# Choosing the last two sequences' experts together, with four of layer 2's early expert blocks between the last pieces of attention

## The chip, the core and the metric

The kernel runs on one core of one Trainium2 chip. The metric is the device time of one execution in microseconds (us). The kernel before took 618.17 us, the median of 9 runs (616.67 to 621.07).

A core has five engines that the text names as the profile does: PE (matrix products; PEld is its weight load), DVE (element-wise work and reductions), ACT (activations and copies), POOL (here: row scatters and a few powers) and SP (issues transfers).

## The reference

2048 tokens of width 128 (8 sequences of 256), everything in f32. The output is a chain of six residual steps:

```python
x = x + 0.5 * ffn(layernorm(x))                # experts, "layer 1" below
x = x + attention(layernorm(x))                # 16 heads of 8
x = x + 0.5 * ffn(layernorm(x))                # the same experts, "layer 2"
x = x + 0.5 * channel_mix(layernorm(x))
x = x + gated_convolution(layernorm(x))
x = x + 0.5 * channel_mix(layernorm(x))
```

The expert step sends each token to the two best of 8 experts:

```python
h = rmsnorm(x @ W_in.T, in_norm_w)
logits = h @ Wr.T
_, idx = top_k(logits + expert_bias, 2)
gates = softmax over the two chosen logits, 0 elsewhere
for e in range(8):
    oe = rmsnorm(silu(h @ Wg[e].T) * (h @ Wu[e].T) @ Wd[e].T, enorm_w[e])
    out = out + gates[:, e] * oe
return rmsnorm(out, out_norm_w) @ W_out.T
```

The inner width of an expert is 512.

## The kernel before

**Tiles.** The tokens are 16 tiles of 128, four to a chunk (`xs[c]`). Sequence b is half of chunk b // 2. An expert layer has three parts: choosing (`dispatch`, L338), the experts' products (`experts`, L679), and weighing the product rows up (`combine`, L807).

**Choosing.** `dispatch(f, i, parts, mp)` returns the steps for one part of layer f: parts are four tiles each in layer 1 (`EARLY`), and 4, 4, 4, 2, 2 in layer 2 (`LATE`, L58). The steps are `turned` (transposes on PE, copy on ACT), `product` (the matrix product with W_in and Wr together, copied by ACT at L383 to `u`, and its squares at L388), `measured` (statistics of x on DVE), `summed` and `inverted` (the factor `ri` of the norm, L392), `logits` (L407), `scaled` (the two row copies `hrow`, ACT L414), `choice` twice (two rounds of six or seven small DVE operations for all tiles of the part, L416), `ranked` (PE products with `tri` and `ones`, which give each token its row), `placed` (positions `posi`) and `rows` (L465): two scatters on POOL per tile, `hs<-hrow,posi_f` at L470, which lay the rows out by expert in DRAM. For the last two parts of layer 2 the factor is a square root on ACT (L398) and a reciprocal on DVE; for the other parts of layer 2 it is a power on POOL (`power_of`, L170).

**Leading blocks.** For every expert, 128 rows are known to be there before all tokens have chosen (`flagged`, L533, after the first 6 or 8 tiles). These are blocks 0 to 7, one per expert: `weights(e)` fetches an expert's weights (832 KB) to a place set by `homes` or to one of four buffers `w_lead`, `read` (L546) fetches the eight row blocks from `hs`.

**The table.** The rest of the rows make up dynamic blocks, pairs (256 rows, 13 or 12 of them) and singles (128). Which expert and which rows each has is worked out on DVE in seven steps (`table`, L564): counted, summed, paired, spared, singled, named, bounded. `named` writes the row and the expert that SP then reads as registers for its fetches; `bounded` gives the bounds `far`.

**Products.** `work` (L782) runs over leading blocks and then `TURNS[f]` (L48): for each block `gate` (four products on PE, silu on ACT into `sg`), `turn_rows` of the next block, `up` (four products, then `hg = pu * sg` on DVE, L738), then a table step, then `down` of the block before (L740): product `py`, squares on ACT (L762), `yrow` on DVE (L763), two DVE operations for `idx`, and a scatter on POOL for each 128 rows (`y<-yrow_f,idx_f`, L769). Fetches of block i + 3 are issued behind block i, rows before weights. `MORE` blocks run only if the input needs them.

**Order.** PE, DVE, ACT and SP run in the order of the program (a manual schedule), and POOL's marked instructions too. Attention runs in steps s of two halves; `at(s, h, …)` puts pieces of other work behind half "a" or "b" of step s. For layer 2's choosing:

```python
at(33, "a", lead["read"], u6, places, partial(rows, [0]))
at(33, "b", root_table, s6, partial(rows, [1]), w(2))
at(34, "a", partial(turn_back, b), partial(rows, [2]), w(4), i6, l6, c6[0])
at(34, "a", partial(turn_heads, b), partial(rows, [3]), w(2), h6, partial(out_heads, b))
at(34, "a", w(2), x7, w(2), m7, c6[1], u7, w(2), s7, r6)
at(34, "a", i7, p6, rows6, l7, *c7, h7, r7, p7, rows7)
at(34, "a", *(partial(lead["weights"], e) for e in (3, 4, 5)))
```

The suffix 6 marks tiles 12 and 13 (the seventh sequence), 7 marks tiles 14 and 15 (the eighth). x is `turned`, u `product`, m `measured`, s `summed`, i `inverted`, l `logits`, h `scaled`, c the two rounds of `choice`, r `ranked`, p `placed`. `turn_back`, `turn_heads` and `out_heads` (L1069 to L1094) are the last pieces of attention for the last sequence; `out_heads` ends with the addition to x at L1094. `w(n)` is n filler products on PE whose result nobody reads. After this, `second_experts` (L937) fetches the last two leading weights and calls `run_experts` (L891): step `counted` first, then `work` with a table step per leading block, with `named` and `bounded` both at block 4.

Of the kernel before, what the change touches and what calls it, by code (L numbers as in the profile page):

```python
# [2 lines left out]

# [13 lines left out]
P = 128  # L17
# [28 lines left out]
LEAD = 6, 8  # L46
LEADING = list(range(NT, NT + E))
TURNS = (  # L48
    [0, 1, 2, 15, 3, 4, 5, 16, 6, 7, 8, 17, 9, 10, 18, 11],
    [0, 1, 2, 15, 3, 4, 5, 6, 16, 7, 8, 9, 17, 10, 11, 12],  # L50
# [6 lines left out]
EARLY = (0, 4), (4, 4), (8, 4), (12, 4)  # L57
LATE = (0, 4), (4, 4), (8, 4), (12, 2), (14, 2)  # L58
# [15 lines left out]
def macaron_kernel(ctx: ExitStack, tc: tile.TileContext, a: dict, out: bass.AP):  # L74
# [70 lines left out]

    root_table()

# [190 lines left out]
    def dispatch(f, i, parts, mp):  # L338
# [5 lines left out]
        paced = f == 1 and i < len(parts) - 2  # L344
# [4 lines left out]
        def turned():  # L349
            pt = bank(f"pxt_{n}", "sa")  # L350
            for t in range(nt):
                nc.tensor.transpose(pt[:, ts(t, P)], x[:, t, :], ident)
            st["xt"] = xntp.tile([P, CT], F32, tag="xnt", name=f"xnt_{n}")
            nc.scalar.copy(st["xt"][:, 0 : nt * P], pt[:, 0 : nt * P])
            st["u"] = mp.tile([P, TPC, D + E], F32, tag="u", name=f"u_{n}")[:, 0:nt]
            st["ss"] = small.tile([P, nt], F32, tag="ss", name=f"ss_{n}")

        def measured():
            bs = small.tile([P, nt, 6], F32, tag="ast", name=f"ast_{n}")
            mv = small.tile([P, nt, 2], F32, tag="amv", name=f"amv_{n}")  # L360
            for t in range(nt):
                nc.vector.bn_stats(bs[:, t, :], x[:, t, :])
            for t in range(nt):
                nc.vector.bn_aggr(mv[:, t, :], bs[:, t, :])
            st["z"] = small.tile([P, nt], F32, tag="z", name=f"z_{n}")
            nc.vector.tensor_scalar(st["z"], mv[:, :, 1], RMS_EPS, RMS_EPS * LN_EPS, ALU.mult, ALU.add)
# [25 lines left out]
        def summed():  # L392
            ri = small.tile([P, nt], F32, tag="ri", name=f"ri_{n}")
            nc.vector.scalar_tensor_tensor(ri, st["ss"], 1.0 / D, st["z"], ALU.mult, ALU.add)
            if f == 0:
                nc.vector.tensor_copy(hrow[:, :, :, D].bitcast(I32), tokid[:, slots])
            if f == 0 or i >= len(parts) - 2:
                nc.scalar.activation(ri, ri, AF.Sqrt)  # L398
            else:
                power_of(ri, ri, mhalf.to_broadcast([P, nt]))  # L400
            st["ri"] = ri

        def inverted():
            if f == 0 or i >= len(parts) - 2:
                nc.vector.reciprocal(st["ri"], st["ri"])
# [59 lines left out]
        def rows(ts_=range(nt)):  # L465
            for t in ts_:
                if paced:
                    nc.vector.tensor_copy(st["posi"][:, t, :], st["pos"][:, t, :])
                for k in range(2):
# [5 lines left out]
                    )  # L475
                    tc.declare_no_dep(ins.ins, group=f"hs{f}", reason="rows of their own")
# [11 lines left out]
        if i < len(parts) - 2:  # L488
            return turned, *halves, measured, summed, logits, scaled, *choices, both(ranked, placed), rows
        return turned, halves[0], measured, summed, inverted, logits, scaled, *choices, ranked, placed, rows  # L490

    def counts(f):
        pc = bank(f"pcnt_{f}", "sb")[:, 0:E]
# [22 lines left out]

    def leading(f, gp, homes, rows, yrows):
# [6 lines left out]
        lead["taken"], lead["base"], lead["masks"], lead["idx"] = flags[:, 0], flags[:, 1], masks, idx  # L524

# [19 lines left out]

        def read():  # L546
# [5 lines left out]
            for e, row in enumerate(first):  # L552
                hst = rows[e].unsqueeze(1)
# [7 lines left out]
        lead.update(weights=weights, flagged=flagged, read=read)  # L561
# [117 lines left out]
    def experts(f, tab, far, y2, mp, pieces, lead):  # L679
# [3 lines left out]
        hst, w = lead["hst"], lead["w"]  # L683

# [3 lines left out]
        def fetch_weights(t):  # L688
# [3 lines left out]
            e = nc.values_load(tab[0:1, 1, t : t + 1], engines=[SP], min_val=0, max_val=E - 1)  # L692
# [47 lines left out]
        def down(t):  # L740
# [27 lines left out]
            for s in range(m):  # L768
# [10 lines left out]
                if t >= NT:  # L779
                    tc.keep_in_program_order(ins)  # L780
# [961 lines left out]
```

## Time and profile before

| what | us |
|---|---|
| median of 9 runs | 618.17 |
| the profiled execution | 616.43 |
| its span in the trace | 614.6 |
| layer 1, choosing (from the start) | 0 to 50 |
| layer 1, eight leading blocks | 51 to 90.9 |
| layer 1, dynamic blocks | 90.9 to 176 |
| combining and attention | 176 to 375.4 |
| layer 2, rest of the choosing | 375.4 to 393.5 |
| layer 2, eight leading blocks | 393.5 to 420.1 |
| layer 2, dynamic blocks | 420.1 to 503.8 |
| last three steps | 504 to 614.6 |

The profile lists busy times of each engine, the span in 40 slices with the granted clock of PE, the chain of waits that ended last, and groups of equal instructions. A line of the timeline is: start, duration, engine, line of the kernel, operation, out<-in, shapes, and in brackets how long the engine had stood idle before it and what ended that. "remote" and "issue" mark idle time for which the trace shows no releasing instruction of the engines it names. Busy over the whole span: PE 518.9 us (84%), DVE 357.4 (58%), ACT 277.7 (45%), POOL 194.0 (32%). The mean granted clock is 0.933 of full speed.

### The profile page before, as it was taken

The numbers are of one execution on the slowest core, as the hardware profiler recorded it, in microseconds if no ns is written. First come the engines' busy times: TensorE is split into PE (matmuls) and PEld (weight loads), VectorE is DVE, ScalarE is ACT, GpSimd is POOL, SyncE is SP. The second block draws the span as 40 slices with busy tenths as digits, with TensorE's granted clock in tenths as the row PEclk, the third lists the DMA queues.
The fourth block names the chain that finished last, engine by engine and source line by source line (L and its number), as shares of the span: only waits on it lengthen the run. The fifth ranks groups of instructions, "written<-read, shape, count | busy, mean of one in ns | idle before, by whom it ended". The sixth has DMA issues, their size and how long they took to land.

```text
span 614.6 us, 11358 instructions
## 1 busy us (share of the span) xinstructions
PE 518.9 (84%) x3954; PEld 402.8 (66%) x3954; DVE 357.4 (58%) x1129; ACT 277.7 (45%) x683; POOL 194.0 (32%) x202
## 2 busy tenths in 40 slices
PE   6325679999978998899899887589999978879996
PEld 5315679889854645555555554589989964558884
DVE  5643555456433666766876885484444432777675
ACT  4524233222223555666665564333323323885365
POOL 0647324575333111101101435522333434410110
PEclk9556699999989999999999999599999998989999
DMA  8823056766513308218026104617667705000002
GB/s 308 347 67 119 27 190 208 214 189 187 195 28 97 54 28 246 90 44 281 24 63 153 52 24 142 255 32 256 192 192 249 220 24 139 2 0 2 1 0 69
DMA packets 37952, 76.96 MB, mean 125 GB/s; under 512 B 4667, under 2 KB 27106, under 8 KB 36608
## 3 DMA queue, kind: packets, MB, share of 16 engines
q1 hardware_dynamic: 33360, 66.62, 35.0%
q0 software_dynamic: 4528, 9.52, 4.4%
q8 instruction: 35, 0.57, 0.4%
q14 instruction: 29, 0.24, 0.1%
HBM read 55.28 MB, written 21.44 MB: 125 GB/s over the span
## 4 chain that ended last, share of the span: by engine, by line
PE 59%; DVE 14%; ACT 10%; DMA 8%; issue 7%; POOL 1%; SPq 0%; DVEq 0%; ACTq 0%; POOLq 0%
PE pg_f L722 9%; PE ps L1127 9%; PE pu_f L722 9%; PE py_f L745 8%; DMA y<-yrow_f,idx_f 5%; PE po L1174 4%; ACT es L1164 3%; PE pvf L1496 2%; PE pgo L1523 2%; DVE m L1147 2%; PE pm L1110 2%; PE pht_f L709 1%; DMA hst_f<-hs 1%; DMA y_f<-y 1%; PE pk_m L1440 1%
## 5 line engine op out<-in xcount | busy, mean ns | idle before, releaser
L1164 ACT ACTIVATE es<-ps 128x1024 f32<-128x1024 f32 x64 | 65.3, 1021 | 53.0 <-PE ps L1127 28.6
L1147 DVE TENSOR_REDUCE m<-pm 128x4 f32<-128x1024 f32 x64 | 77.5, 1220 | 12.6 <-PE pm L1110 12.6
L1127 PE MATMUL ps<-qa,qk 32*128 32x256 f32 x512 | 72.8, 401 | 12.0 <-ACT es L1164 8.6
L738 DVE TENSOR_TENSOR hg_f<-pu_f,sg_f 128x1024 f32<-128x1024 f32 (+1 forms) x48 | 46.5, 969 | 62.1 <-PE pu_f L722 38.5
L470 POOL DMA_INDIRECT hs<-hrow,posi_f x64 | 61.7, 964 | 62.9 <-issue 25.7
L769 POOL DMA_INDIRECT y<-yrow_f,idx_f x57 | 56.1, 984 | 80.3 <-issue 45.4
L1110 PE MATMUL pm<-qk 32*128 32x256 f32 x512 | 73.2, 400 | 0.6 <-ACT qk L1057 0.6
L731 ACT ACTIVATE sg_f<-pg_f 128x1024 f32<-128x1024 f32 (+1 forms) x48 | 39.3, 819 | 58.9 <-PE pg_f L722 35.3
L762 ACT ACTIVATE ysq_f<-py_f 128x128 f32<-128x128 f32 x73 | 19.7, 274 | 100.0 <-PE py_f L745 84.3
L1127 PEld LDWEIGHTS ps<-qa,qk 32*128 32x128 f32 x512 | 43.7, 184 | 30.0 <-ACT es L1164 21.0
L745 PE MATMUL py_f<-w_f,hg_f 128*128 128x128 f32 x456 | 56.7, 276 | 2.0 <-DVE yrow_f L763 2.0
L745 PEld LDWEIGHTS py_f<-w_f,hg_f 128*128 128x128 f32 x456 | 54.9, 192 | 3.6 <-DVE yrow_f L763 2.3
L722 PE MATMUL pg_f<-ht_f,w_f 128*128 128x256 f32 (+1 forms) x256 | 54.9, 357 | 0.7 <-DMA w_f<-in_wall_dram 0.7
L722 PE MATMUL pu_f<-ht_f,w_f 128*128 128x256 f32 (+1 forms) x256 | 54.7, 357 | 0.0
L722 PEld LDWEIGHTS pg_f<-ht_f,w_f 128*128 128x128 f32 x256 | 42.9, 191 | 4.7 <-DVE hg_f L738 0.9
L1110 PEld LDWEIGHTS pm<-qk 32*128 32x128 f32 x512 | 44.3, 184 | 2.6 <-issue 1.5
L722 PEld LDWEIGHTS pu_f<-ht_f,w_f 128*128 128x128 f32 x256 | 43.0, 191 | 4.5
L171 POOL TENSOR_TENSOR cf_f<-cf_f,mhalf 128x8 f32<-128x8 f32 (+1 forms) x9 | 13.5, 1502 | 65.8 <-DVE cf_f L834 64.2
L1174 PE MATMUL po<-es,v 128*32 128x256 f32 x512 | 34.3, 385 | 0.0
L763 DVE TENSOR_TENSOR yrow_f<-py_f,w_f 128x256 f32<-128x256 f32 (+1 forms) x32 | 12.7, 396 | 37.0 <-ACT ysq_f L762 34.4
L1159 DVE TENSOR_TENSOR qa<-pmt,qk 128x256 f32<-128x256 f32 x32 | 13.5, 422 | 25.7 <-PE pmt L1153 25.5
L714 DVE TENSOR_SCALAR ht_f<-pht_f,pack 128x256 f32<-128x256 f32 (+1 forms) x32 | 14.5, 453 | 16.6 <-PE pht_f L709 13.7
(327 smaller groups left out, 992.1 us busy)
## 6 DMA issues: line engine op xcount, KB each, us to landing
w_f<-in_wall_dram SPq DMA_DIRECT2D x32, 832.0 KB
hs<-blank SPq DMA_DIRECT2D x8, 1032.0 KB
qk<-in_wall_dram SPq DMA_DIRECT2D x7, 832.0 KB
w_lead<-in_wall_dram SPq DMA_DIRECT2D x7, 832.0 KB
y_f<-y SPq DMA_DIRECT2D x14, 258.0 KB
hst_f<-hs SPq DMA_DIRECT2D x25, 129.0 KB
pack<-in_pack_dram SPq DMA_DIRECT2D x1, 1729.0 KB
v<-in_wall_dram SPq DMA_DIRECT2D x2, 832.0 KB
```

Source lines behind the costliest of these rows:

```text
L470: ins = nc.gpsimd.indirect_dma_start(out=hss[f], out_offset=bass.IndirectOffsetOnAxis(ap=st["posi"][:, t, k : k + 1], axis=0), in_=hrow[:, ...
L722: nc.tensor.matmul(ph[:, k, :], w[t][:, o + k * P : o + k * P + P], ht[t], start=True, stop=True)
L731: nc.scalar.activation(sg, pg, AF.Silu)
L738: nc.vector.tensor_mul(hg[t], pu, sg)
L745: nc.tensor.matmul(py[:, s, :], hg[t][:, k, ts(s, P)], w[t][:, 2 * DFF + k * D : 2 * DFF + k * D + D], start=(k == 0), stop=(k == NFC - 1),)
L762: nc.scalar.activation(sq[:, s], py[:, s], AF.Square, accum_out=yrow[:, s, D : D + 1])
L769: ins = nc.gpsimd.indirect_dma_start(out=y2, out_offset=bass.IndirectOffsetOnAxis(ap=idx[:, s : s + 1], axis=0), in_=yrow[:, s, :], in_off ...
L1110: nc.tensor.matmul(sc[:, jj, i, :], qs[c][r, g, col + i * P : col + (i + 1) * P], ks[c][r, g, col : col + S], start=True, stop=True,)
L1127: nc.tensor.matmul(sc[:, jj, i, :], ks[c][r, g, col + i * P : col + (i + 1) * P], tops[s][r, :], start=True, stop=True,)
L1147: nc.vector.tensor_reduce(m, sc, AX.X, ALU.max, negate=True)
L1164: nc.scalar.activation(es, sc, AF.Exp, scale=scale)
L1174: nc.tensor.matmul(po[32 * j : 32 * j + 32, :], vs[c][:, (b % 2) * 2 + i, (g % 2) * (H // 2) + (g // 2) * 4 + j, :], ess[s, j // 2][:, j % ...
```

## The change

1. In layer 2 the last four tiles are one part. `turned`, `product`, `measured`, `summed` and `scaled` still run for two tiles at a time; logits, choices, ranks, positions and rows run once for four. The factor comes from POOL's power; the square-root table load goes, and a silu table load takes a place ahead of the begun blocks. The fillers `w(n)` go.
2. Leading blocks 0 to 3 of layer 2 (`BEGUN = 4`) run between these pieces, with small buffers of their own; `hg` takes the place of `sg`. Their four product rows are sent behind the last row scatter (`issue_after`).
3. Table steps: in layer 1 one per block, `named` at block 4 and `bounded` at block 5 (before, both at block 4); in layer 2, which has four leading blocks left in the loop, two per block in the first three. Dynamic fetches wait for the last step's place in the program; the first dynamic block's weights are fetched ahead of its rows.
4. The indices of all leading blocks are worked out at once at block 0 in a few DVE operations (before, two per block); a dynamic block's ahead of its product row.
5. Both loops end with a single block instead of a pair (the same blocks in another order).
6. In layer 1 all eight leading weights are fetched at the start (before, seven; the eighth when a buffer came free), and product rows and the table's scratch lie elsewhere.

```diff
+BEGUN = 4
 TURNS = (
-    [0, 1, 2, 15, 3, 4, 5, 16, 6, 7, 8, 17, 9, 10, 18, 11],
-    [0, 1, 2, 15, 3, 4, 5, 6, 16, 7, 8, 9, 17, 10, 11, 12],
+    [0, 1, 2, 15, 3, 4, 5, 16, 6, 7, 8, 17, 9, 10, 11, 18],
+    [0, 1, 2, 15, 3, 4, 5, 6, 16, 7, 8, 9, 10, 11, 12, 17],
 )
-EARLY = (0, 4), (4, 4), (8, 4), (12, 4)
-LATE = (0, 4), (4, 4), (8, 4), (12, 2), (14, 2)
+PARTS = (0, 4), (4, 4), (8, 4), (12, 4)
...
-            if f == 0 or i >= len(parts) - 2:
+            if f == 0:
                 nc.scalar.activation(ri, ri, AF.Sqrt)
             else:
-                power_of(ri, ri, mhalf.to_broadcast([P, nt]))
-            st["ri"] = ri
+                power_of(ri, ri, mhalf.to_broadcast([P, hi - lo]))
...
-        return turned, halves[0], measured, summed, inverted, logits, scaled, *choices, ranked, placed, rows
+        steps = turned, measured, summed
+        ends = [
+            (halves[b], partial(scaled, (2 * b, 2 * b + 1)), *(partial(step, 2 * b, 2 * b + 2) for step in steps))
+            for b in range(2)
+        ]
+        return *ends, logits, *choices, ranked, placed, rows
...
+    def number(out, rows, keep, set_):
+        nc.vector.tensor_tensor(out, rows[:, :, D].bitcast(I32), keep, ALU.bitwise_and)
+        nc.vector.tensor_tensor(out, out, set_, ALU.bitwise_or)
...
+        def numbers():
+            o = 0
+            for ap, n in rows:
+                got = ap.rearrange("p (e r) -> p e r", r=ROW)
+                number(idx[:, o : o + n], got, masks[:, 0, o : o + n], masks[:, 1, o : o + n])
+                o += n
...
-        def work(turns, pieces):
-            n = len(turns)
-            for t in turns[:3]:
-                fetch_weights(t)
-                fetch_rows(t)
+        def work(turns, pieces, ready=0):
+            n, asked = len(turns), 0
+            def ask(upto, i):
+                nonlocal asked
+                while asked < min(upto, n) and (turns[asked] >= NT or i >= ready):
+                    first = turns[asked] == TURNS[f][0]
+                    for fetch in (fetch_weights, fetch_rows) if first else (fetch_rows, fetch_weights):
+                        fetch(turns[asked])
+                    asked += 1
+            ask(3, 0)
...
-                    down(turns[i - 1])
-                if i + 3 < n:
-                    fetch_rows(turns[i + 3])
-                    fetch_weights(turns[i + 3])
-            down(turns[-1])
+                    down(turns[i - 1])()
+                ask(i + 4, i)
+            down(turns[-1])()
...
-        tab, far, steps = table(f, pc, gp, lead, scratch)
+        lead["tab"], lead["far"], steps = table(f, pc, gp, lead, scratch)
         steps[0]()
-        steps = [*steps[1:5], both(*steps[5:7])]
-        steps += [lambda: None] * (E - len(steps))
+        m = len(turns)
+        k = -(-6 // m) if m < 6 else 1
+        steps = [both(*steps[o : o + k]) for o in range(1, 7, k)]
+        ready = len(steps) - 1
+        steps += [lambda: None] * (m - len(steps))
+        lead["tiles"].work(turns + TURNS[f], steps + pieces, ready)
...
-            for e in range(7):
+            for e in range(E):
                 lead["weights"](e)
...
+                def send_begun():
+                    with tc.issue_after(latest["scatter"]):
+                        for send in sends:
+                            send()
...
+                T, G, U, Y = (partial(partial, f) for f in (turn_lead, gate_lead, up_lead, down_lead))
                 b = B - 1
-                at(32, "a", w(3))
                 at(32, "b", x6, m6)
                 at(33, "a", lead["read"], u6, places, partial(rows, [0]))
-                at(33, "b", root_table, s6, partial(rows, [1]), w(2))
-                at(34, "a", partial(turn_back, b), partial(rows, [2]), w(4), i6, l6, c6[0])
-                at(34, "a", partial(turn_heads, b), partial(rows, [3]), w(2), h6, partial(out_heads, b))
-                at(34, "a", w(2), x7, w(2), m7, c6[1], u7, w(2), s7, r6)
-                at(34, "a", i7, p6, rows6, l7, *c7, h7, r7, p7, rows7)
+                at(33, "b", s6, partial(rows, [1]), silu_table)
                 at(34, "a", *(partial(lead["weights"], e) for e in (3, 4, 5)))
+                at(34, "a", partial(turn_back, b), T(0), partial(rows, [2]), h6, G(0))
+                at(34, "a", partial(turn_heads, b), T(1), U(0), partial(out_heads, b), G(1), x7)
+                at(34, "a", U(1), m7, u7, Y(0), s7, partial(rows, [3]), T(2), G(2), Y(1), l67, c67[0])
+                at(34, "a", U(2), T(3), G(3), c67[1], Y(2), r67, h7, p67, rows67, counted)
+                at(34, "a", U(3), Y(3), send_begun)
...
-            return run_experts(1, counts(1), gp, lead, scratch, [])
+            return run_experts(1, lead["pc"], gp, lead, scratch, LEADING[BEGUN:], [])
```

T, G, U and Y are `turn_rows`, `gate`, `up` and `down` of a begun block; `l67` to `rows67` are the steps for four tiles.

## The prediction

> **What bounds the kernel now.** I read the 40 slices first: where PE is busy it is PE that sets the time, and the thin slices show where it is something else. Then the stage table over 355 to 420 us, the chain of waits there, the timelines of POOL, SP and PE, and the waits of PE around the other places that the diff touches.
>
> ```profile
> PE   6325679999978998899899887589999978879996
> ...
> PEclk9556699999989999999999999599999998989999
> ...
> PE 59%; DVE 14%; ACT 10%; DMA 8%; issue 7%; POOL 1%; SPq 0%; DVEq 0%; ACTq 0%; POOLq 0%
> ```
>
> The first row is PE's busy share in slices of 15.4 us, the second its granted clock. The 26th slice (384.1 to 399.5) is the choosing of layer 2's last experts, with the clock at half. The third row, the chain's shares, says that over the whole span PE holds 59% of the chain, DVE 14% and waits for nothing visible 7%. Stage by stage (PE, PEld, DVE, ACT, POOL busy, granted clock, DMA share, GB/s):
>
> ```profile
> 355.00:375.40 20.40, 17.98 (x203) 10.80 (x200) 15.38 (x62) 11.97 (x21) 8.79 (x9) 1.00 0.08 27
> 375.40:385.60 10.20, 6.08 (x28) 3.28 (x28) 4.63 (x25) 4.05 (x9) 7.44 (x8) 1.00 0.81 246
> 385.60:399.30 13.70, 8.84 (x38) 8.33 (x39) 6.39 (x38) 4.35 (x12) 7.87 (x9) 0.50 0.60 240
> 399.30:420.10 20.80, 19.08 (x168) 18.70 (x167) 15.41 (x61) 7.83 (x25) 5.91 (x6) 1.00 0.34 107
> ```
>
> Between 375.4 and 393.4 the end is set by a chain of small DVE operations; PE's work there is fillers and transposes. From 393.46 (first gate of a leading block) to 420.1 PE sets it, cold until 399.3. The chain of waits shows what stands in the first stretch:
>
> ```profile
> 381.73 0.17 DVE mask_f L435
> 381.90 4.49 issue
> 386.39 0.16 DVE ri_f L394
> 386.56 0.09 DVE ahead L444
> ```
>
> 4.49 us of "issue": the product feeding `ri_f` ended at 381.53, and the copy that reads it began 3.7 us later:
>
> ```profile
> 385.25 0.39 ACT L383 COPY u_f<-pin_f 128x272 f32<-128x272 f32 x1 [4.50 <-remote]
> ...
> 399.06 0.69 DVE L738 TENSOR_TENSOR hg_f<-pu_f,sg_f 128x512 f32<-128x512 f32 x1 [4.74 <-remote]
> ...
> 64.89 0.69 DVE L738 TENSOR_TENSOR hg_f<-pu_f,sg_f 128x512 f32<-128x512 f32 x1 [13.04 <-issue]
> ```
>
> The other two are alike: their products ended 1.6 and some 10 us earlier. All three fall late in a run of back-to-back row scatters on POOL (376.0 to 385.8, 389.1 to 398.9, 43.7 to 64.9; one each 1.26 us). I know no more than this coincidence; call it the hold.
>
> **The middle of layer 2.** Work removed from PE's time: blocks 0 to 3 move between the attention pieces. A leading block at full clock is gate 0.89, transpose 0.11, up 0.89, down 0.89 = 2.8 us; four are 11.2 us, and PE has room for them from 375.4 to 393.4 (9.1 busy of 18, mostly fillers that go). So if PE alone bounded, some 11 us plus the cold loss would fall away. It doesn't: the first dynamic block needs its table, and I add the rows along each engine's order.
>
> Choosing. Four tiles now choose together, so the chain starts only when both sequences are there. The square root on ACT and reciprocal on DVE (0.19 + 0.16 us) become a power on POOL (1.02 to 1.06 in its rows), queued behind two scatters: the first ends near 379.4. What the program puts behind it waits too: on ACT the scaling and block 0's silu, on DVE block 0's `hg` and then the attention's additions. The last `x` add, now 379.52, comes at about 382.4; products at 384.8 (now 381.5); the four-tile logits at 389.8 (now 388.2), since 2 × 13 choice operations of 0.2 us become 13, partly giving back the delay; the mask at 393.8 (now 391.2); the count at about 395.9 (now 392.3).
>
> Table. Its DVE operations take 9.4 us by rows (counted 1.1, summed and paired 2.7, spared and singled 2.1, named and bounded 3.4). Now they lie in blocks 0 to 5, first step at 393.2, last at 411.53. After, the first step stands on DVE behind the products and scalings of block 3, about 399.5; then DVE is nearly full with the table and the `hg` 0.69 and `mul` 0.29 of four blocks, less 4 × 0.31 for indices, which now take a few operations at block 0. End: 410.9. SP then issues the first weights at 411.6 and the rows at 412.8 (now rows 412.18, weights 413.37; 1.2 us each). An early weights row took 3.9 us (379.50 to 383.4); so weights and rows are there at 415.6. PE's order then has the transpose with its copy to SBUF (some 0.6), block 7's up (0.89) and block 6's down (0.89) before the gate: 417.8 to 418. Now the dynamic gates start at 420.11: **−2.3 us**. PE has nothing left from about 410.3 to 415.7: the leading blocks, which covered the table, are used up.
>
> That gap is 5.4 us. Before, PE stood idle from 381.96 to 385.69 and the clock was 0.50 from 385.6 to 399.3; other cold spells (505.1, 518.8, 542.6) last 3.4 us. I charge one such spell, 3.4 us at half speed less what overlaps waiting: **+1.4**. The Trainium skill, "TensorE: Matmul & The Clock Gate", section "HAM oscillation — how this bites in real kernels", gives the rule of no PE-idle gaps over some 3.4 us and says that a longer one starts the next work at half clock. The 3.7 us idle agrees. The rule speaks against this change, which takes the fillers out and makes a longer gap; by it the loss is surer than by the row, of the same size. Net for the middle: −2.3 + 1.4 = −0.9. From both sides: −4.5 (table without DVE crowding, 2.2 earlier, and no cold spell) to +6.4 (the slower rival below).
>
> The four y scatters of the begun blocks are issued after the last row scatter: a run of 12, some 397.4 to 412.8. In themselves they delay nothing that PE reads before the layer's end; the next y scatters (now 404 to 419) only queue. The silu table load, 1.28 us on ACT, merely changes place: now at 393.42, with no PE wait behind it.
>
> **Layer 1's leading blocks.**
>
> ```profile
> PE py_f L745 <- DVE v L763: 1.5, 1, 1.5
> PE pg_f L722 <- DMA w_lead<-in_wall_dram: 1.1, 1, 1.1
> PE pg_f L722 <- DMA w_f<-in_wall_dram: 0.7, 1, 0.7
> ```
>
> These three waits of PE, at 80.6, 86.0 and 90.2, are 3.27 us (1.51, 1.05, 0.70 in the timeline). With all eight weights fetched at the start the second goes; the table's last step one block later softens the first. Late next: the first dynamic weights, whose buffer is free and whose table entry is known around 83.3; now 85.00 after rows at 83.31, landed 90.9 (5.9 us). Weights before rows brings them up to 1.2 us forward, but the rows come behind. The dynamic gate moves from 90.91 to between 88.4 and 91.4: I take **−1.0**, bounds −2.5 to +0.5. One weight more before the start (0.83 MB) moves into slices of DMA share 0.8; it is the eighth to be used, so nobody waits.
>
> **The ends of the loops.** A single block now comes last. Layer 1 now ends with a pair: `down` starts at 173.00, its two scatters at 177.18 and 178.46, end 179.43. With a single at the end the last product row needs one square (0.27) less, and one scatter (1.28) less stands at the very end; but the pair's two scatters are just ahead of it in POOL's queue and PE's wait of 0.79 for the last `hg` stays. **−0.9** (−1.3 to −0.3). Layer 2: last scatters at 504.81 and 506.10, end 507.08; a single's row is there near 504.0 less the shorter `down` of 0.89; the pair's scatters have gone by 503.9, end 505.8: **−1.3** (−2.2 to −0.4). The combining reads behind them move as much (182.69 and 509.49 now). Dynamic blocks now work out their indices ahead of the product row instead of behind it: the row's `mul` comes some 0.3 later, the scatter not, and PE, which by then is in the next block's gate, sees nothing; if that cover were gone it would be 0.3 for a single block.
>
> **Sum.** −1.0 − 0.9 − 0.9 − 1.3 = −4.1. The profiled execution took 616.43 (span 614.6 and 1.83 around it), so 612.3 there. It lies 1.74 below the median 618.17 of the nine runs; the forecast for the median is **614.1**, 0.7% faster. A measurement tells about 0.3% from no change, here 1.85 us.
>
> **Rivals.**
>
> *The hold takes the table.* The run of 12 scatters lasts longer than either 8-run now, and the table falls in its second half. If a product is read 3.7 us late there, as the copy was at 385.25, the table ends near 414.6, 3.7 later: 617.8. For: every hold began after some seven scatters of a run. Against: many runs' operations went unharmed, and DVE's small operations read no PE product. 0.18.
>
> *Slower.* The hold strikes both runs. The first (376 to 385.6) stands over the power, the `x` add and the products, now all on one chain of four tiles, with gates and downs of blocks queued in between on the same engines: in program order, whatever is held holds the choosing. Priced at 2.6 there (midway between the 1.6 and 3.7 above) and at 4.7 (the 399.06 row's idle) in the second: +7.3 over the forecast, 621.4. It decides from the point where the table ends 5.9 us after 410.9, at 416.8. For: the chain now passes POOL and interleaves with blocks. Against: the long row of 4.5 is in the 616.43 already, and goes if the copy falls behind the run's end, as I put it. 0.25.
>
> *Better.* No hold where the choosing now is, DVE not crowded, the gap short of a cold spell: another 3.6 off, 610.5. 0.15.
>
> *It doesn't do what it says.* Weights 3 (landed 383.4) or the rows come so late that the early blocks bunch behind the choosing as now; the middle gives nothing: 615.0, within the forecast's side.
>
> **How the numbers follow.** Forecast and its near misses (612 to 616.3) 0.42, better 0.15, hold 0.18, slower 0.25. Faster 0.57, same 0.18, slower 0.25. The range starts at 608.5, the better case with 2 us of the 2.8 us by which the low bounds of layer 1 and the two ends lie under the values I took (1.5, 0.4, 0.9), and reaches to 621.5, which just takes in the slower rival's price; some 0.05 lies below it and 0.15 above.
>
> **What would show it.** After: PE busier at full clock from 376 to 393; the last `x` add near 382.4; a first table step near 399.5 and last near 410.9; first dynamic weights issued ahead of rows near 411.6; a dynamic gate near 417.8 behind an idle of PE and a clock of 0.50; 12 back-to-back scatters, and whether a copy or `hg` behind a finished product names "remote". In layer 1 no wait for `w_lead`. At the loops' ends one scatter, not two, behind the last `down`. The prediction is wrong if the table ends after 414, if the gate follows the leading blocks with no gap, or if the clock falls in the choosing itself.

## The result

The changed kernel took 628.09 us, the median of 10 runs (623.91 to 631.76); the kernel before took 618.07 in 31 runs (615.03 to 622.89). The ratio is 1.0154, interval 1.013 to 1.0178: 1.5% slower, where 0.7% faster was forecast and the range ended at 621.5. The profiled execution took 630.16 us, its span is 628.4 (616.43 and 614.6 before). All ratios in this text are of fast runs only; one of the six runs of E3 below was a slow one.

The same rows of the page and of the stage table as in the prediction, now for the changed kernel:

```profile
PE   6314779999969999899898888767999988889996
...
PEclk9557699999979999999999996877999998989999
...
PE 31%; issue 14%; ACT 10%; DVE 6%; DMA 5%; POOL 5%; SPq 0%; POOLq 0%; DVEq 0%; ACTq 0%
```
```profile
355.00:375.40 20.40, 16.91 (x200) 10.68 (x202) 16.85 (x65) 11.50 (x19) 9.04 (x10) 0.98 0.09 28
375.40:385.60 10.20, 8.74 (x47) 4.89 (x39) 2.12 (x13) 4.79 (x12) 3.82 (x5) 0.50 0.37 87
385.60:399.30 13.70, 11.32 (x83) 10.62 (x84) 5.27 (x24) 5.95 (x20) 7.15 (x8) 0.90 0.82 333
399.30:420.10 20.80, 14.25 (x79) 12.70 (x78) 9.07 (x38) 3.95 (x11) 11.64 (x12) 0.75 0.12 38
```

PE's clock is at half from 375.4 to 385.6, where it was 1.00, and not full afterwards. From 399.3 to 420.1, where PE worked through the leading blocks (19.08 of 20.8 us busy), it is now busy for 14.25.

Events of both traces, as differences, say where the time went (`es` are attention's exponentials and `osb` its copies, both on ACT). The last column has the same differences on a second chip, which the first experiments met:

| stretch | forecast | first chip | second chip |
|---|---|---|---|
| start to layer 1's first dynamic gate (90.91, now 94.37) | −1.0 | +3.46 | +3.17 |
| from there to attention's first `es` (206.98, now 211.05) | −0.9 | +0.61 | +0.05 |
| attention, to its last copy `osb` (375.39, now 383.36) | 0 | +3.90 | +1.33 |
| choosing and table, to layer 2's first dynamic gate (420.11, now 435.96) | −0.9 | +7.88 | +7.80 |
| from there to the end of the span | −1.3 | −2.05 | −1.15 |
| sum | −4.1 | +13.8 | +11.2 |

Only the last term came. (A single profile: the medians differ by 10.0 on the first chip and, as shown below, 12.75 on the second.)

In layer 1 PE waits for rows that stand behind weights in SP's queue (both fences from the changed kernel):

```profile
90.83 0.44 PE L747 MATMUL pht_f<-ident,hst_f 128*128 128x128 f32 x2 [4.30 <-DMA hst_f<-hs]
```
```profile
84.57 0.33 SPq L733 DMA_DIRECT2D w_f<-in_wall_dram  x1
86.20 1.56 SPq L741 DMA_DIRECT2D hst_f<-hs  x2
```

Weights are issued at 84.57, when block 4's buffer is free (SP has waited 3.8 us for it), and only then the rows at 86.20; before, rows went at 83.31 and weights at 85.00. PE needs the rows first, for the transpose. So the three waits of 3.27 us became one of 4.30, and the work behind it ran cold: 1.91 us for the next `down` instead of 1.06.

In layer 2 DVE's table shows the rest (a line of DVE's timeline: start, duration, operation, and in brackets its idle time before and what ended it):

```profile
408.58 0.16 DVE L621 TENSOR_TENSOR tab_cnt<-pcnt,lflags 128x8 f32<-128x8 f32 x1
...
413.83 0.69 DVE L779 TENSOR_TENSOR hg_f<-pu_f,sg_f 128x512 f32<-128x512 f32 x1 [4.11 <-issue]
...
422.07 0.69 DVE L779 TENSOR_TENSOR hg_f<-pu_f,sg_f 128x512 f32<-128x512 f32 x1 [4.83 <-remote]
...
428.62 0.18 DVE L686 TENSOR_SCALAR tab_far<-tab_free 128x48 int32<-128x48 f32 x1
```

I had DVE nearly full from the first step at 399.5 to the last at 410.9. It took from 408.6 to 428.8, 20.2 us: it stands idle for 4.11 and 4.83 us inside the table, each time in front of an `hg`. The changed kernel on the second chip has the first of the two idle times and not the second:

```profile
383.72 0.15 DVE L621 TENSOR_TENSOR tab_cnt<-pcnt,lflags 128x8 f32<-128x8 f32 x1
...
388.97 0.69 DVE L779 TENSOR_TENSOR hg_f<-pu_f,sg_f 128x512 f32<-128x512 f32 x1 [4.12 <-PE pu_f L761]
...
392.30 0.69 DVE L779 TENSOR_TENSOR hg_f<-pu_f,sg_f 128x512 f32<-128x512 f32 x1
...
398.90 0.18 DVE L686 TENSOR_SCALAR tab_far<-tab_free 128x48 int32<-128x48 f32 x1
```

There the table takes from 383.7 to 399.1, 15.4 us. The 4.1 us are a wait for PE; the 4.83 are a hold, as the prediction calls it, of the first chip.

### The profile page after: what moved, and what is told of

The parts are those of the page before. It is cut to its first block, busy times and chain, and to the rows that moved or that the text cites. A ratio compares the mean times of both kernels' runs of the same rounds, so it can differ in the third digit from the quotient of the medians.

```text
span 628.4 us, 11263 instructions
## 1 busy us (share of the span) xinstructions
PE 525.7 (84%) x3936; PEld 409.0 (65%) x3936; DVE 350.4 (56%) x1081; ACT 276.4 (44%) x680; POOL 196.0 (31%) x204
## 4 chain that ended last, share of the span: by engine, by line
PE 31%; issue 14%; ACT 10%; DVE 6%; DMA 5%; POOL 5%; SPq 0%; POOLq 0%; DVEq 0%; ACTq 0%
PE ps L1190 8%; POOL y L812 4%; PE po L1237 3%; ACT es L1227 3%; DMA y<-yrow_f,idx_f 2%; PE pvf L1573 2%; PE pgo L1600 2%; DVE m L1210 2%; DMA qk<-heads 2%; PE pm L1173 2%; PE pk_m L1517 1%; ACT xn_m L1482 1%; PE pr_m L1499 1%; PE pqk L1097 1%; PE warm_y L202 1%
## 5 line engine op out<-in xcount | busy, mean ns | idle before, releaser
L779 DVE TENSOR_TENSOR hg_f<-pu_f,sg_f 128x1024 f32<-128x1024 f32 (+1 forms) x44 | 43.7, 994 | 67.1 <-PE pu_f L761 39.8
L1237 PE MATMUL po<-es,v 128*32 128x256 f32 x512 | 35.8, 399 | 0.0
```

The costliest lines, as they stand in the source:

```text
L779: nc.vector.tensor_mul(hg[t], pu, sg)
L1237: nc.tensor.matmul(po[32 * j : 32 * j + 32, :], vs[c][:, (b % 2) * 2 + i, (g % 2) * (H // 2) + (g // 2) * 4 + j, :], ess[s, j // 2][:, j % ...
```

## The experiments

They ran on several chips, which the record numbers: E1 to E6 and the two unchanged kernels beside them on chip 1, E7 to E10 on chip 0, F1 to F4 on chip 5, G1 and G2 on chip 3. The kernel before takes 589.6 to 590.2 us on chips 1, 3 and 5, and 619.6 on chip 0; the chip of the result, where it takes 618, has no number on record. By these times the text calls chips 1, 3 and 5 together the second chip, and chip 0 and that of the result the first. Each version is compared with the kernel before on its own chip, in the same session.

**Fillers put back.** E1 gives attention's steps 32 and 33 their fillers again:

```diff
+at(32, "a", w(3))
 at(32, "b", x6, m6)
-at(33, "b", s6, partial(rows, [1]), silu_table)
+at(33, "b", s6, partial(rows, [1]), silu_table, w(2))
```

> The changed kernel with the removed fillers put back at two places only: three 128-column products in the first half of step 32, two in the second half of step 33. Nothing else differs. Theory (the clock fell in the last steps of attention because these fillers went): granted clock 1.00 up to about 380 instead of 0.50 from 375.4 to 385.6; the last attention copy osb, 383.4 in the changed kernel, comes at about 380 (its delay against the kernel before falls from 8.0 to 4.6 us), and the time falls by 3 to 4 us, to about 624.5. Rival (the begun blocks themselves, put between the pieces, make the delay, and the clock only follows the thinner work): clock still at half there, osb within 0.7 us of 383.4, time within 1 us of the changed kernel.

**Rows first.** E2 fetches the first dynamic block's rows ahead of its weights:

```diff
-first = turns[asked] == TURNS[f][0]
-for fetch in (fetch_weights, fetch_rows) if first else (fetch_rows, fetch_weights):
+for fetch in (fetch_rows, fetch_weights):
```

> The changed kernel, with the first dynamic block's rows fetched ahead of its weights again, in both layers. Theory (in layer 1 the rows, queued behind weights that wait for a buffer, hold the first dynamic block: PE waited 4.30 us for hst at 90.8 and its clock then fell): the wait for hst falls below 1 us, the first dynamic gate of layer 1 comes near 91 instead of 94.4, time lower by 3 us, about 625; in layer 2 no difference above 0.5 us, since weights and rows are both asked for only at 426.5 to 427.8. Rival (what is late is the weights, since the buffer they need comes free only when block 4 is done): PE then waits for w_f instead, first gate at 93 or later, time lower by less than 1.5 us.

**Sends apart.** E3 sends each begun block's rows where they are ready (`tiles.down(NT + t)()` in place of `sends.append(...)`, and no `send_begun`).

> The changed kernel, with the four product rows of the begun blocks sent where they are ready, in program order, instead of in one run behind the eight last row scatters. Theory (a long back-to-back run of scatters on POOL holds the other engines from about its sixth or seventh scatter on): the last run is 9 scatters instead of 12 and ends some 3.8 us earlier; the waits of 5 us before hg at 422.07 and before sg at 418.44 shrink or go, the table's last step, now 428.7, ends near 422 to 425, time lower by 3 to 6 us, 622 to 625. Rival (the table is late because DVE and ACT have to work through four begun blocks first, at half clock): table end within 1 us of 428.7, time within 1 us. A third: a product row not ready in time holds POOL's queue and with it the row scatters, so that the rows are late: time higher.

**Loop ends alone.** E4 is the kernel before with the new `TURNS` and nothing else.

> The kernel before with one part of the change alone: both loops of dynamic blocks end with a single block. Theory (as predicted, one scatter and a shorter product row stand behind the last down): first read of y in layer 1 0.9 us earlier, in layer 2 1.3 earlier, time lower by 2 us, about 616. Rival (seen in the profile of the changed kernel: the single's scatter queues behind the pair's two, and PE waits 1.18 us for the last hg product and 3.81 us at the loop's end, long enough for its clock to fall): layer 1's end no earlier or up to 1 us later, layer 2's end 1 us earlier, time within 1 us of before.

Measured, with the unchanged kernels run on the same chip afterwards:

| version | us | ratio to before (interval) |
|---|---|---|
| before | 589.7 | |
| changed | 602.42 | 1.0223 (1.0188 to 1.0257) |
| E1 fillers back | 598.93 | 1.0159 (1.0126 to 1.0192) |
| E2 rows first | 597.51 | 1.0106 (1.0070 to 1.0142) |
| E3 sends apart | 601.69 | 1.0170 (1.0130 to 1.0211) |
| E4 loop ends alone | 591.64 | 1.0037 (1.0017 to 1.0056) |

> The kernel before, unchanged, for its profile on the chip of the first four experiments, where it takes 589.7 us and not 618. Theory (the idle stretches in which a copy or an hg started 4 to 13 us after its product belong to the first chip, not to long runs of scatters): none of them here, first leading gate of layer 1 near 41.5 instead of 51.0 and first down near 47 instead of 65.6, and layer 2's choosing 4 us shorter. Against its own times, the version that ends both loops with a single block shows where it loses 2 us: at layer 1's end.

> The changed kernel, unchanged, timed and profiled beside the kernel before on this chip. Theory (its loss is made of rows queued behind weights in layer 1, a clock at half in the last steps of attention, and a table that stands on DVE behind the begun blocks' hg; the held operations of the first chip add little to the difference): slower by 1.5 to 2.2%, 599 to 602 us. Rival (the held operations in the run of 12 scatters make the loss): without them no slower than 0.5%, below 593.

E2 gains 4.9 us by the medians, and its theory holds: rows are issued at 60.83 instead of 63.19, layer 1's first dynamic gate is at 69.05 (before 68.67, changed 71.84), and PE's only wait there is now for weights:

```profile
69.05 1.97 PE L761 MATMUL pg_f<-ht_f,w_f 128*128 128x256 f32 x8 [1.93 <-DMA w_f<-in_wall_dram]
```

The profiles show 2.8 us of the gain at this gate and 0.9 from there to the first `es`; where the rest lies they don't show (E2's runs spread from 591 to 599). E1 gains 3.5 us, as expected. What its two fillers do is seen beside the changed kernel on the same chip, here PE's timeline at the end of attention, first changed, then E1:

```profile
348.93 0.44 PE L1216 MATMUL pmt<-ident,m 128*128 128x128 f32 x2
350.39 1.13 PE L1190 MATMUL ps<-qa,qk 32*128 32x256 f32 x8 [1.03 <-DVE mx_f L433]
351.45 1.92 PE L1237 MATMUL po<-es,v 128*32 128x256 f32 x16
```
```profile
350.47 0.81 PE L202 MATMUL warm_e<-pack,ident 128*128 128x384 f32 x2
351.66 1.13 PE L1190 MATMUL ps<-qa,qk 32*128 32x256 f32 x8 [0.38 <-DVE mx_f L433]
352.73 1.07 PE L1237 MATMUL po<-es,v 128*32 128x256 f32 x16
```

Without the 0.81 us of filler the 16 products `po` take 1.92 instead of 1.07: behind a gap of 1.03 us, the longest of PE in the 50 us before, the clock falls (0.67 on the mean from 350 to 354.5; in E1 it is 1.00 over the same products). From the first `es` to `osb` the changed kernel, E2 and E3 need 170.6, 173.1 and 173.3 us, E1 and the kernel before 169.4 and 169.3.

E3's theory falls, for this chip: the run of 12 scatters becomes one of 9, and nothing moves beyond the intervals. Here no operation is held at all (the prediction's three lines have no counterpart in any of the traces), so E3 says that the run costs nothing by itself here. On the first chip the table's delay against `osb` is the same as here (the end of `named` is 7.65 us later there, 7.91 here), because the kernel before lost some 5 us to holds there as well. So the holds don't make the difference between the two kernels.

E4 is slower by 2 us where 2 were to be gained; its rival had both places right, but not the time. Layer 2's end does gain 0.9 us (from the first dynamic gate to the end of the span); layer 1 loses 1.05 from its first dynamic gate to the first `es`. There is PE behind the loop, first in the kernel before, then in E4, on the same chip:

```profile
155.39 1.74 PE L197 MATMUL warm_f<-pack,ident 128*128 128x512 f32 x4 [2.60 <-DVEq L804]
157.12 2.05 PE L290 MATMUL ptf<-filt,pack 128*128 128x128 f32 x16
```
```profile
157.29 3.10 PE L197 MATMUL warm_f<-pack,ident 128*128 128x512 f32 x4 [3.56 <-ACT dec L283]
160.18 2.32 PE L290 MATMUL ptf<-filt,pack 128*128 128x128 f32 x16
```

The idle time before the fillers is 3.56 instead of 2.60, and they run at half clock, 3.10 instead of 1.74 us. These two ends nearly cancel. The rest of the difference of the two profiles (0.55 before the loop, 0.3 in attention, 0.8 in layer 2's choosing) stands where the two kernels are the same; single profiles scatter by as much, but the medians differ by 2 us too, and why isn't shown.

**Both undone, and fewer begun blocks.** E5 has E1's and E2's edits. E6, E7 and E8 have them too, and begin two, three and no blocks in attention (`BEGUN`, and the T, G, U, Y of the others taken out of the places; the table's steps go two to a block with five or six blocks, one with eight).

> The changed kernel with two of its edits undone together: fillers in steps 32 and 33, and rows ahead of weights for the first dynamic block. Theory: the gains add up, 4.5 us of layer 1 and 2 to 4 us of layer 2 against the changed kernel, and what is left of the loss is the table behind the begun blocks: 594 to 596 us, against 589.7 before. Rival (one of the two gains is eaten by the next wait, since the choosing is bound elsewhere): within 1.5 us of the version with rows first alone, 597.5.

> The same two edits undone, and two leading blocks begun inside attention instead of four; the six that are left in the loop carry the table's steps two by two as before. Theory (DVE reaches the table late because it stands in program order behind the hg and product rows of begun blocks 2 and 3 and of block 4, and then too few leading blocks are left to cover it): the first table step follows the count within 1 us instead of 6, the first dynamic gate comes 3 to 6 us earlier than with four, time 589 to 592. Rival (each begun block saves its PE time, so fewer of them is worse): 2.8 to 5.6 us slower than with four, 598 to 601.

E5: 592.17 us, 1.0029 (1.0009 to 1.0049), better than the 594 to 596 expected. Together the two edits give 10.25 us of the 12.75; alone they gave 4.9 and 3.5, and the 1.9 us more lie within the intervals. What is left is choosing and table: from `osb` to the first dynamic gate 45.28 us, in the kernel before 39.40; behind that gate E5 is faster. E6: 587.36, 0.9961 (0.9936 to 0.9986), better than the 589 to 592 expected, with 39.83 us there. DVE's lines of E5 and of E6:

```profile
374.50 0.69 DVE L779 TENSOR_TENSOR sg_f<-pu_f,sg_f 128x512 f32<-128x512 f32 x1 [1.88 <-PE pu_f L761]
377.88 0.29 DVE L807 TENSOR_TENSOR m<-py_f,qk 128x128 f32<-128x128 f32 x1 [2.69 <-ACT ysq_f L806]
378.09 0.15 DVE L621 TENSOR_TENSOR tab_cnt<-pcnt,lflags 128x8 f32<-128x8 f32 x1
...
383.34 0.69 DVE L779 TENSOR_TENSOR hg_f<-pu_f,sg_f 128x512 f32<-128x512 f32 x1 [4.12 <-PE pu_f L761]
```
```profile
370.49 0.17 DVE L621 TENSOR_TENSOR tab_cnt<-pcnt,lflags 128x8 f32<-128x8 f32 x1
...
375.45 0.69 DVE L779 TENSOR_TENSOR hg_f<-pu_f,sg_f 128x512 f32<-128x512 f32 x1 [3.87 <-PE pu_f L761]
```

In E5 the count's product starts at 371.96 and the table's first step reads it at 378.09, behind `hg` and product row of block 3 (1.88 + 2.69 us of idling). In E6 these are 369.86 and 370.49. The 4 us in front of the next `hg` are in both: it waits for the first block after the choosing, at half clock. So what E6 wins is the first step, 0.6 us behind the count instead of 6.1; the table itself takes as long (15.1 us, in E5 15.4). E6's table has named the rows at 383.68, and rows and weights are there when PE has finished block 7; in E5 PE waits 2.9 us for the rows.

> Fillers and rows first put back, and three leading blocks begun in attention; the version with four took 592.2 us, with two 587.4, before 589.7. Theory (what costs is DVE's order: the table stands behind hg and product row of the blocks begun last, and the loop has too few leading blocks left to cover it): between the two, 588.5 to 591; first table step 1 us behind the count as with two, since block 2's down is done by then, but five blocks cover the table instead of six, so PE waits 1 to 2 us for the first dynamic rows. Rival (only the fourth block does harm, by its up and down behind the count): as fast as two or faster, 584.5 to 587.

> Fillers and rows first put back, and no leading block begun in attention; all eight follow the choosing, one table step per block, which still is done for four tiles at once. Theory (a begun block saves PE time only while the table stays covered, two do, four don't): PE works through 8 blocks of 2.8 us behind the choosing, 5.6 us more than with two, of which the shorter choosing gives 1 to 2 us back: 589.5 to 592.5, about the kernel before. Rival (begun blocks hold the choosing so much that none at all is best): below 587.

These two met the first chip: E7 614.34, 0.9922 (0.9896 to 0.9947), E8 615.32, 0.9925 (0.9899 to 0.9952). Their expected times were for the other chip, and E6 wasn't run on this one, so the order among two, three and none isn't settled. By ratio both lie in their rivals' ranges (585 us on a chip of 589.7): I had expected each at about the kernel before, and both are 0.8% under it, with no difference between them that can be measured. From `osb` to the gate E7 needs 46.61 us there and E8 45.55, the kernel before 44.72, so their gain isn't made by begun blocks but in layer 1 (88.67 and 87.72 instead of 90.91 at the first dynamic gate) and behind layer 2's first dynamic gate (192.5 and 191.0 us to the end of the span instead of 194.5).

**Fillers in the choosing; the loop's end.** E9 adds fillers to E6:

```diff
-at(34, "a", ..., Y(1), l67, c67[0])
-at(34, "a", c67[1], r67, h7, p67, rows67, counted)
+at(34, "a", ..., Y(1), fresh("warm_g", 4), l67, c67[0])
+at(34, "a", fresh("warm_h", 4), c67[1], fresh("warm_i", 2), r67, h7, p67, rows67, counted)
```

> The version with two begun blocks (587.4 us), with fillers on PE in its choosing as well: four products behind the second down, four and two more around the second round of choices. Theory (PE stands idle for 3.89 us before the ranks, and its first 3.4 us behind them run at half clock, which delays hg of block 2 and with it the table): clock 1.00 over the first leading block in the loop, its gate 1.16 instead of 2.08 us, first dynamic gate 1.5 to 2 us earlier, 585 to 586. Rival (DVE, with the table, is what bounds these blocks): gate faster, but the first dynamic gate within 0.5 us, time the same.

> The same as the last, with layer 1's loop ending in a pair again (the kernel before's order) and layer 2's in a single. Theory (in layer 1 the single at the end brings nothing: the wait of PE behind the loop grows from 2.6 to 3.3 us and more, and its clock falls): 0.5 to 1 us faster than the last. Rival (the single gives 0.9 us there too): 0.5 to 1 us slower.

On the first chip E9 takes 612.5 us, 0.9887 (0.9853 to 0.9921), E10 612.79, 0.9890 (0.9854 to 0.9926): in layer 1 the single at the end is worth nothing either way. E9 on the second chip (G2):

> Two begun blocks with the fillers there, in steps 32 and 33, and rows first, beside the run above, for the second chip. Where before takes 590: theory (PE at half clock behind the choosing was the limit of the first blocks in the loop) 585 to 586.5, ratio 0.992 to 0.995; rival (DVE's table) 587.4 as without the fillers. Where before takes 619: ratio 0.989 again.

586.34 us, 0.9937 (0.9919 to 0.9955). The time came, but not by its mechanism, and its interval overlaps E6's: the gate of block 2 still runs cold,

```profile
372.39 2.07 PE L761 MATMUL pg_f<-ht_f,v 128*128 128x128 f32 x8 [0.46 <-ACT ht_f L750]
```

although no idle of PE before it is longer than 1.16 us (in E6 it was 3.89 us). Between the last filler, which ends at 368.5, and this gate PE has only four short groups of products, with waits of 0.2 to 1.0 us around them. From `osb` to the first dynamic gate G2 needs 39.43 us, 0.4 less than E6, where 1.5 to 2 were expected.

No version is shorter than the kernel before in the stretch that this part of the change is about, from `osb` to layer 2's first dynamic gate: 39.83 and 39.43 us against 39.40 on the second chip, 45.27 (E10) to 46.96 (E9) against 44.72 on the first. The versions that are faster than before win elsewhere. For E6 that is 1.2 us in attention and 2.6 behind the gate, of which E4 shows 0.9 as the loop's end; the rest of it was not taken apart.

**Breaking the runs of scatters.** F1 is the changed kernel with an unused power of 0.7 us on POOL after every second scatter of the run of 12, F2 the kernel before with it after every second row scatter, F3 E9 with both, F4 the kernel before with a memset of 0.1 us instead.

> The changed kernel with a power of two elements per row on POOL (0.7 us, its result is not used) after every second scatter of the run of 8 row scatters and 4 product rows behind layer 2's choosing. Theory (on the chip where the first profile was taken, copies and hg are held late in long back-to-back runs of scatters, and a run that is broken holds nobody; the changed kernel's run of 12 cost it 5 us before sg at 418.44, hg at 422.07): where the kernel before takes some 618, no operation waits over 2 us for a finished product there, first dynamic gate 3 to 6 us earlier, time 3 to 6 us lower than 628 (ratio to before 1.005 to 1.010). Where before takes some 590, no hold to lose and POOL's run 4 us longer: time within 1 us of 602.4. Rival (the hold has to do with that chip and not with runs): no gain on either.

> The kernel before with the same pause after every second row scatter, in both layers and all parts. Theory (runs): where before takes some 618, the holds of layer 1 go (copy at 40.28, hg at 64.89) and the first dynamic gate of layer 1 comes 10 to 20 us earlier than 90.9, time 8 to 18 us lower; where it takes some 590, the choosing of layer 1 lasts up to 4 us longer on POOL, of which little is seen: 589 to 594. Rival (the chip, not runs): 618 or more, with the same waits. A third (the pause moves the start of the hold but not its length): the operations held are others, time within 3 us.

> Two begun blocks, fillers there and in steps 32 and 33, rows first, and the pause after every second row scatter and every second product row of the begun blocks. Theory (runs): ratio to before lower than the 0.9887 that it has without the pauses on the chip of 619.6, by what the kernel before gains from them there; 0.988 to 0.996 on the chip of 590. Rival (the chip): 0.988 to 0.993 on the one, 0.992 to 1.0 on the other.

> The kernel before with a shorter pause in the same places: one memset of a column, 0.1 us. Theory (what counts is that another instruction stands between the scatters): the same gain as with 0.7 us. Rival (what counts is the time in which POOL issues no scatter): less than a third of that gain, or none.

> The kernel before with a pause of 0.7 us on POOL after every second row scatter, once more, for the case that it meets the chip on which before takes some 618 us. Theory (held operations belong to unbroken runs): there the waits at 40.28 and 64.89 of layer 1 go, first dynamic gate of layer 1 at 75 to 85 instead of 90.9, time 600 to 612. Rival (they belong to the chip): the same or later holds there, 620 to 630. On the chip of 590: 600, as measured, and the question stays open.

All met chips on which nothing is held: F1 601.94, 1.0204 (1.0180 to 1.0229); F2 600.21, 1.0168 (1.0150 to 1.0187), again as G1 599.27, 1.0161; F3 597.47, 1.0155, outside both of its ranges; F4 590.11, 1.0013 (0.9991 to 1.0034). Whether the holds of the first chip belong to unbroken runs stays open. F2 missed its expectation for these chips: POOL's 33 scatters in layer 1's choosing are not off the path. Its first dynamic rows are issued at 71.28 instead of 61.02, and its first dynamic gate is at 78.81 instead of 68.67: that is the loss.

## Why the prediction was wrong, point by point

- **What bounds.** Right that DVE's chain and the table set the time there and that PE's savings would not come through. Wrong that PE's work between the pieces was fillers that could go at no cost: they carried the clock. Put back alone they are worth 3.5 us on the second chip. I had charged the clock only for the gap behind the table and put attention's term at 0; it is +3.9 and +1.3. On my list of what would make the prediction wrong stood a fall "in the choosing itself"; it fell before it.
- **Clock.** The Trainium skill, "TensorE: Matmul & The Clock Gate", section "HAM oscillation — how this bites in real kernels", warns of idle gaps over some 3.4 us. The fall after 1.03 us of idling says that this is not the whole condition here. The same page's section "A second HAM failure mode: psum-queue depth-cycling" says that in one kernel frequent short idles between groups of products switch the clock; the trace agrees that short idles can, but no run here shows by which rule.
- **Choosing.** The last `x` add came 2.6 us later against `osb` (forecast 2.9), the mask 2.4 (2.6): these terms were right on the first chip. The two powers take 0.7 us each, not 1.02 to 1.06; the first stands behind two scatters as forecast, the second behind 4.3 us of idle POOL.
- **Table.** The failing step: "then DVE is nearly full with the table and the `hg`". The first step stood 3.6 us behind the count by forecast and 5.0 in the trace (5.6 on the second chip, 6.1 in E5), and from the first step to the last it took 20.2 us on the first chip and 15.4 on the second instead of 11.4. I had added DVE's busy times, and added them short (9.4 + 4 × 0.98 − 4 × 0.31 is 12.1). In program order the first `hg` between the steps waits 4.1 us for PE, on both chips; PE runs cold there (clock 0.54 from 378 to 388 us on the second chip) and in its turn waits for DVE (T of block 4 needs the bank, the place for its product, that the count's product leaves only with the first table step: 0.92 us). The other 4.8 us of the first chip are a hold. E6, with two blocks fewer in front, takes the first step's delay away, and of the 5.9 us that E5 needs more than the kernel before in this stretch all but 0.4 are gone; the wait inside the table stays, with more blocks left to cover it.
- **A saving that wasn't there.** The −0.9 compares a forecast of 42.4 us from `osb` to the gate, 43.8 with the cold spell and without any hold, with 44.72 us of the kernel before, which has some 5 us of holds. Where nothing is held the kernel before needs 39.40, so the prediction's own working comes to a loss of over 4 us there.
- **Layer 1.** "Weights before rows brings them up to 1.2 us forward, but the rows come behind" was the mechanism, and I sized it from −2.5 to +0.5; it is +3.2 to +3.5. What I left out: the rows don't wait 1.2 us for an issue but for the weights' buffer, and that buffer is free only after block 4. E2, with the rows first again, is back within 0.4 us of the kernel before at this gate.
- **Loop ends.** Layer 2's −1.3 came (−0.9 in E4, −1.15 and −2.05 in the changed kernel). Layer 1's −0.9 didn't come: in E4 PE waits longer behind the loop and its clock falls, and E10, with the pair put back there, is as fast as E9.
- **Rivals.** The slower rival had its place right, the interleaving in program order, and 0.25; its price of 621.4 was made of holds, which are not the cause. "The hold takes the table" (0.18) was right that one would fall into the table on this chip, 4.83 us, but the kernel before has its own there. The run of 12 scatters does nothing that can be measured where nothing is held.

Of 12.75 us on the second chip, undoing the order of rows and weights and the lost fillers gives back 10.25 (4.9 and 3.5 alone). Two begun blocks instead of four give another 4.8, which takes the time 2.3 us below the kernel before, so this part cost more than the 2.5 us that were left: the rest of the change gains some. With the first two undone and two blocks begun the change is faster than before on the second chip; with fillers in the choosing as well it is on both, 0.9937 and 0.9887. On the first chip E1, E2, E5 and E6 weren't run; there the split rests on the table of differences and on E7 to E10.

## What to carry to other kernels

Before interleaving work between the pieces of a critical chain, write out every engine's order and put a start time on each instruction; a sum of busy times misses the idling that the interleaving itself creates. Before taking out fillers, look at the clock in the stretch that they stand in and at what is thin around it. When a fetch is moved ahead of another in one queue, ask what the moved one still waits for.

## What the runs showed that I had not expected

- Chips differ by 28 us on the same program (618 to 620 on chip 0 and on that of the result, 590 on chips 1, 3 and 5), and nearly all of it lies where operations are held: first leading gate of layer 1 at 51.03 and 41.54, first dynamic gate at 90.91 and 68.67; from `osb` to layer 2's first dynamic gate 44.72 and 39.40. The stretches between take the same time within 1 us. In all six profiles of the first chip a copy on ACT stands idle for 6.6 to 7.3 us before it starts near 40 us and an `hg` for 10 to 13 before it starts near 63, with no releaser in the trace; in the 14 profiles of the second no ACT or DVE instruction has such an idle time over 2 us. What holds them is not settled. Unbroken runs of 33 scatters hold nobody on the second chip. The prediction tied one chip's holds to long runs, on a coincidence, and priced its rivals by them.
- PE's clock fell where its longest idles were 1.03 and 1.16 us, among thin products, and fillers of 0.81 us avoided the one but 2.8 us of them did not avoid the other.
